# VectorE's two-operand pieces in an image loop, rewritten as scalar_tensor_tensor

## The chip, the cores and the metric

The kernel runs on one NeuronCore of one Trainium2 chip. A core has five engines that run side by side, each through its own list of instructions in order: TensorE (PE, matrix products; PEld is its weight load), VectorE (DVE), ScalarE (ACT), GpSimd (POOL) and SyncE (SP), which here only issues transfers between HBM and the on-chip memory SBUF. TensorE writes its results to a second on-chip memory, PSUM. The metric is the device time of one execution in microseconds, lower is better.

## The reference

Sixteen images of 64 x 64 pixels with 128 channels go through two layers. Layer 0 is a deformable resampling: a group norm, a 3 x 3 convolution that gives two offsets for each channel and pixel, a clip of the resulting coordinates to the image, and a bilinear sample of the normalised image there. Layer 1 is an attention among the 16 numbers of each head of each token, and a mixture of experts whose gate takes the eight best tokens of each of 64 experts.

```python
x = x + conv_ref(_gn(x), L0_conv_W, L0_conv_b)
#   c0 = clip(off[..., 0] + row, 0, 63); c1 = clip(off[..., 1] + col, 0, 63); bilinear sample
t = _to_tokens(x)
t = t + attn_ref(_ln_t(t), w_qkv, b_qkv, w_proj, b_proj)
#   attn = softmax((q * scale)[..., :, None] * k[..., None, :]); out = attn . v, head by head
t = t + ffn_ref(_ln_t(t), gate_w, gate_b, weight1, weight2)
#   softmax over tokens, the 8 best of each expert, two dense layers, added back to those tokens
```

## The kernel before, in words

All arithmetic is in float32, apart from some small bfloat16 pieces of the coordinates. Channels or tokens lie on the 128 partitions. The program is one long piece for the first image, a loop over the fourteen images between (`For_i`, line 1070), a piece for the last image, and then `finish`, which computes the experts and adds their outputs. The change touches only the images' part.

An image is worked in eight strips of 512 pixels. For each strip the following runs:

- `conv(k)` makes the coordinates: 18 matmuls into `cbank` (lines 617 to 623), `coords` adds bias and grid on VectorE (630 to 637), `clip` bounds both coordinates to 0..63 (644), ScalarE and GpSimd split the row coordinate into three bfloat16 parts (645 to 656), and SyncE stores the column coordinate to `cc_d` (646) and the parts to `pc_d` (658).
- `sample` is the heart: 16 steps a strip, 128 an image. In each, SyncE loads `chat` from `cc_d` in four transfers (697), TensorE makes `rps` (719) and ScalarE turns it into row weights `rhat` (728, 729; on VectorE in one step of eight, 726), ScalarE turns `chat` into column weights (708), TensorE makes `yps` in 64 small matmul passes from the image's rows `xr` (739), VectorE multiplies, `product` (745), and TensorE sums into `acc` (751). `yps` has one buffer, so each step's matmuls wait for the product of the step before.
- `tokens` carries a finished strip through the attention: transposes, query, key and value (`qkv`, 852), the extremes of the keys `kmm` (860), GpSimd's `top` and `den` (865), VectorE's maximum `top` (904), GpSimd's `sc` = q k and `sc` - `top` (878, 879), ScalarE's exponential (883), VectorE's sum `den` (885), GpSimd's weighting `ev` (889), VectorE's sum `att` (891). Then comes the projection, a layer norm whose `scale` writes `xln` (782), and the gate.
- `prep` brings in the next image: transposes, group statistics in `gmv` (541 to 551), eight `normalize` pieces that write `pad` (557), differences along the rows, `along` (570, 574), and down the columns, eight `down` pieces that write `xl` (583) and are stored to `xn_d`.
- `tail` treats the image before: the eight best tokens (`best`, 957; `choose`, 969, which is already a scalar_tensor_tensor with both tensor operands in SBUF), their weights, and a running sum copied to `pooled` (1024).

Nothing of this is issued where it is written. Each piece is recorded with a slot number, and `Work.order` (237 to 296) plans one image: it gives each operation an estimated cost (`weight`, 195) and repeatedly takes the operation that can start first, ready ones being ranked by start time plus 150 per slot. What it finds becomes the fixed order of each engine's list. The plan also has a rule for the memory port of VectorE and GpSimd: an operation that `shared` (224) marks starts no earlier than the last planned GpSimd operation ends, and the other way round. Marked are VectorE operations with two wide operands in SBUF, and tensor_scalar and tensor_copy from SBUF to SBUF. Because all the recorded operations are emitted from line 188, the profile shows them all as L188, and they are told apart by the names of their tiles.

Of the kernel before, what the change touches and what calls it, by code (L numbers as in the profile page):

```python
# [44 lines left out]
def bcast(ap, axis, n):  # L45

    shape = list(ap.shape)
    return ap.unsqueeze(axis).to_broadcast(shape[:axis] + [n] + shape[axis:])


def at_image(ap, b):
# [89 lines left out]
class Work:  # L141
# [52 lines left out]
    def weight(self, op):  # L194
        total, cells, shape = 0, {}, None
        for fn, outs, ins in op.operands():
            n = max(a.free_size() for a in outs + ins)
            local = all(a.space == SBUF for a in outs + ins)
            if op.lane == "tensor":
                n = ins[1].free_size() if fn == "matmul" else P  # L200
                n = n * (1 if ins[0].dtype == BF16 else 2 if fn == "transpose" else 4) * 0.4
                shape = (ins[0].partition_size(), outs[0].partition_size())
                part = shape[0] <= 64 and fn == "matmul"
                at = (region(ins[0])[1] if part else 0, region(outs[0])[1])
                cells[at] = cells.get(at, 0) + n + 15
                continue
            if op.lane == "sync":
                total += 100
            elif op.lane == "scalar":
                total += 155 + 0.83 * n + 100 * (len(ins) - 1)  # L210
            elif op.lane == "gpsimd":
                total += 1000 if n <= NA else 150 + (6 if fn == "tensor_scalar" else 1.8) * n
            elif fn == "reciprocal":
                total += 6.5 * n
            elif fn in ("tensor_scalar", "tensor_copy") and local:
                total += 150 + 0.55 * n
            else:
                total += 150 + 1.04 * n
        if op.lane == "tensor":
            wide = shape[1] > 64 or shape[0] > 64 and shape[1] > 32  # L220
            total = sum(cells.values()) if wide else max(cells.values())
        return total, shape

    def shared(self, op):

        if op.lane != "vector":
            return False
        for fn, outs, ins in op.operands():
            wide = [a for a in ins if a.space == SBUF and a.free_size() > 1]
            if len(wide) > 1 or (  # L230
                fn in ("tensor_scalar", "tensor_copy")
                and all(a.space == SBUF for a in outs + ins)
            ):
                return True
        return False
# [66 lines left out]
class Images:  # L302
# [8 lines left out]
    def __init__(self, ctx, tc, x, conv_w, conv_b, w_qkv, b_qkv, w_proj, b_proj, gate_w, gate_b,  # L311
# [63 lines left out]

        self.half = keep([P, NA], "half")
        nc.vector.memset(self.half, -0.5)
        self.one = keep([P, 1], "one")
        nc.vector.memset(self.one, 1.0)

# [124 lines left out]
    def prep(self, b, turns, slot, norm_slot):  # L505
        plan = Work(self.nc, self.tc)
        nc = plan
        xt = at_image(self.x, b).rearrange("b r w c -> (b r w) c").rearrange(
            "(t a p) c -> t p a c", a=NA, p=P)

        def load(t):
            nc.sync.dma_start(self.xl[:, t % 2], xt[t])

        def turn(t):
            for a in range(NA):
                nc.tensor.transpose(
                    self.bank2[:, P * a : P * (a + 1)], self.xl[:, t % 2, a, :], self.ident)

        def stats(t):
            v = self.big[:, CHW * t : CHW * (t + 1)]  # L520
            nc.scalar.copy(v, self.bank2)
            nc.vector.bn_stats(self.gst[:, t, :], v)

        for t, at in enumerate(turns):
            plan.add(at - 3, lambda t=t: load(t))
            plan.together(at + 0.5, lambda t=t: turn(t))
            plan.add(at + 1, lambda t=t: stats(t))

        gmv = self.gmv

        def group1():
            nc.vector.bn_aggr(gmv[:, 0:2], self.gst)

        def group2():
            nc.tensor.matmul(self.bank2[:, 0:2], self.avg, gmv[:, 0:2], start=True, stop=True)

        def group3():
            nc.vector.tensor_copy(gmv[:, 2:4], self.bank2[:, 0:2])  # L540
            nc.vector.tensor_tensor(gmv[:, 0:1], gmv[:, 0:1], gmv[:, 2:3], ALU.subtract)
            nc.vector.tensor_tensor(gmv[:, 1:2], gmv[:, 0:1], gmv[:, 0:1], ALU.mult)

        def group4():
            nc.tensor.matmul(self.bank2[:, 0:1], self.avg, gmv[:, 1:2], start=True, stop=True)

        def group5():
            nc.vector.scalar_tensor_tensor(
                gmv[:, 3:4], self.bank2[:, 0:1], GN_EPS, gmv[:, 3:4], ALU.add, ALU.add
            )  # L550
            nc.gpsimd.tensor_tensor(gmv[:, 3:4], gmv[:, 3:4], self.half[:, 0:1], ALU.pow)

        for i, fn in enumerate((group1, group2, group3, group4, group5)):
            plan.add(slot + i + 0.5 * (i % 2), fn)

        def normalize(t):
            nc.vector.tensor_scalar(
                self.pad[:, 1 + 8 * t : 9 + 8 * t, 1 : 1 + IMG],
                self.big[:, CHW * t : CHW * (t + 1)].rearrange("p (i j) -> p i j", j=IMG),
                gmv[:, 2:3], gmv[:, 3:4], ALU.subtract, ALU.mult,  # L560
            )


        pin = self.pad[:, 1 : 1 + IMG, 1 : 1 + IMG]
        big = self.big.rearrange("p (i j) -> p i j", j=IMG)
        mid = IMG // 2

        def along(s):
            if s == 0:
                nc.vector.tensor_tensor(  # L570
                    big[:, :, : mid - 1], pin[:, :, : mid - 1], pin[:, :, 1:mid], ALU.subtract)
                nc.scalar.copy(big[:, :, mid - 1 : mid + 1], pin[:, :, mid - 1 : mid + 1])
            else:
                nc.vector.tensor_tensor(
                    big[:, :, mid + 1 :], pin[:, :, mid + 1 :], pin[:, :, mid : IMG - 1],
                    ALU.subtract)

        def down(r):
            st = self.xl[:, r % 2].rearrange("p a c -> p (a c)").rearrange(
                "p (i j) -> p i j", j=IMG)  # L580
            lo, hi = 8 * r, 8 * (r + 1)
            last = hi == IMG
            nc.vector.tensor_tensor(
                st[:, : 8 - last], big[:, lo : hi - last], big[:, lo + 1 : hi + 1 - last],
                ALU.subtract)
            for n, w in enumerate(ROW0):
                i0, i1 = max(lo, w), min(hi, w + WIN - 1)
                if i0 < i1:
                    nc.sync.dma_start(
                        self.xn_d[:, i0 - w : i1 - w, n], st[:, i0 - lo : i1 - lo])  # L590
                if lo <= w + WIN - 1 < hi:
                    nc.sync.dma_start(self.xn_d[:, WIN - 1, n], big[:, w + WIN - 1])

        for t in range(NCH):
            plan.add(norm_slot + t // 2, lambda t=t: normalize(t))
            plan.add(norm_slot + 6 + 2 * t, lambda t=t: down(t))
        for s in range(2):
            plan.add(norm_slot + 4 + s, lambda s=s: along(s))
        return plan
# [12 lines left out]
    def conv(self, k, slot):  # L612
# [28 lines left out]
            )  # L641

        def clip():
            nc.vector.tensor_scalar(self.cd, self.cd, 0.0, float(IMG - 1), ALU.max, ALU.min)
            nc.scalar.copy(self.pc[:, 0], self.cd[:, 0])
            nc.sync.dma_start(self.cc_d[k % 2], self.cd[:, 1])

# [120 lines left out]
    def layer_norm(self, src, dst, plan, slot):  # L768
# [10 lines left out]
            nc.gpsimd.tensor_tensor(rstd, rstd, self.half, ALU.pow)  # L779

        def scale(a):
            nc.vector.tensor_scalar(
                dst[:, a, :], src[:, a, :], mv[:, a, 0:1], rstd[:, a : a + 1],
                ALU.subtract, ALU.mult,
            )

        for a in range(NA):
# [7 lines left out]
    def tokens(self, b, k, slot):  # L795
# [14 lines left out]
        def add(rel, fn):  # L810
            plan.add(slot + rel, fn)
# [86 lines left out]
        for a in range(NA):  # L898
# [2 lines left out]
            add(at + 8, lambda: qkv_add(a))  # L901
            add(at + 9, lambda: ends(a))
            add(at + 10, lambda: scores(a))
            add(at + 11, lambda: nc.vector.tensor_tensor(
                tile_of(top, a), tile_of(top, a), tile_of(den, a), ALU.max))
            for i in (2 * a, 2 * a + 1):
                add(12 + 4 * i, lambda: score(i))
                add(14 + 4 * i, lambda: expo(i))
# [42 lines left out]
    def tail(self, b, slot, turns):  # L951
# [3 lines left out]

        def best():
            nc.vector.max(self.top8, logits)
            nc.vector.tensor_scalar(self.ntop, self.top8[:, 0:1], -1.0, None, ALU.mult)

        def expo(k):  # L960
            ks = slice(CHW * k, CHW * (k + 1))
# [56 lines left out]
        def keep(i):  # L1018
# [2 lines left out]
            else:  # L1021
                nc.vector.tensor_tensor(self.pool_sum, self.bank2[:, :E], self.pool_sum, ALU.add)
            if i == NCH // 2 - 1:
                nc.vector.tensor_copy(
                    self.pooled[:, :, b : b + 1] if isinstance(b, int)
                    else self.pooled[:, :, ds(b, 1)], self.pool_sum.unsqueeze(2))

# [247 lines left out]
```

## Time and profile before

| what | value |
| --- | --- |
| median of three runs | 10401.05 us (10379.56 to 10412.2) |
| the profiled execution | 10408.53 us, span 10406.5 us |
| granted TensorE clock, mean | 0.912 |
| one image in the loop | about 611 us |
| VectorE busy | 8475.8 us in 11691 instructions |
| GpSimd busy | 7911.5 us in 5666 instructions |
| `finish`, from about 9900 us on | about 500 us |

How to read the lines: a group line has the source line, the engine, the operation, out<-in by tile names, the shape and count, then after the bar the busy time in us and the mean ns of one, and then the engine's idle time just before such instructions with what ended it. A line of the waits gives the engine and what waited, what it waited for, and then us in total, number and longest. A line of the timeline has the start, the duration, the engine and the instruction. A line of a stretch has its borders and length, then the busy time and count of PE, PEld, DVE, ACT and POOL, the granted clock, the share of the DMA engines and GB/s.

### The profile page before, as it was taken

Reading aid. Unit: us, or ns where it says so; the run is one execution under the profiler, and the core shown is the slowest. Engines: PE = TensorE matmul, PEld = TensorE weight load, DVE = VectorE, ACT = ScalarE, POOL = GpSimd, SP = SyncE. Lnnn points to the kernel's source line nnn. Section 1 sums busy time; section 2 is a strip of 40 time slices with the busy share of each in tenths; the row PEclk is TensorE's granted clock in tenths of the full one; section 3 lists DMA queues with packets and bytes.
Section 4 is the critical chain, followed back from the end, with each engine's and each line's share of the span. In section 5 each row is a group of like instructions: output and inputs, shape, how many; then the busy total and the mean of one; then the engine's idle time right before and its main releaser. Section 6 shows DMA issues by size and latency. Waiting matters only on the chain. (4 is left out here: it accounts for less than half of the span.)

```text
span 10406.5 us, 367626 instructions
## 1 busy us (share of the span) xinstructions
PE 8673.1 (83%) x156228; PEld 4367.3 (42%) x156228; DVE 8475.8 (81%) x11691; ACT 7657.4 (74%) x8034; POOL 7911.5 (76%) x5666
## 2 busy tenths in 40 slices
PE   7978788797878889788888978788897878888567
PEld 3434344343434434343443434344343434434247
DVE  5988889888888988888898888889888888988712
ACT  5878788787878878787887878788787878878500
POOL 3978788787878878787887878788787878878700
PEclk9999899998989999999999999999998999999755
DMA  6565555555555555555555555555555555555277
GB/s 160 160 166 157 159 159 158 160 161 163 158 158 159 153 161 159 163 160 160 158 154 161 159 162 161 158 152 156 164 160 159 162 158 154 157 163 157 79 213 247
DMA packets 1325857, 1672.20 MB, mean 161 GB/s; under 512 B 441632, under 2 KB 658464, under 8 KB 1322080
## 3 DMA queue, kind: packets, MB, share of 16 engines
q1 hardware_dynamic: 1303904, 1613.24, 54.4%
q10 hardware_dynamic: 20224, 34.61, 0.9%
q8 instruction: 1244, 20.38, 0.9%
q14 instruction: 485, 3.97, 0.1%
HBM read 1378.16 MB, written 268.96 MB: 158 GB/s over the span
## 5 line engine op out<-in xcount | busy, mean ns | idle before, releaser
L188 DVE SCALAR_TENSOR_TENSOR prod<-chat,yps 128x1024 f32<-128x1024 f32 x2048 | 2470.7, 1206 | 552.7 <-PE yps L188 254.6
L188 PE MATMUL yps<-rhat,xr 32*32 32x176 f32 (+1 forms) x131072 | 2621.3, 282 | 347.7 <-DVE prod L188 324.8
L188 POOL TENSOR_TENSOR ev<-sc,qkv 128x1024 f32<-128x1024 f32 x1024 | 2429.5, 2373 | 546.3 <-ACT sc L188 484.2
L188 PEld LDWEIGHTS yps<-rhat,xr 32*32 32x32 f32 x131072 | 1860.2, 106 | 1692.0 <-DVE prod L188 926.2
L188 PE MATMUL cbank<-pad,wconv 128*128 128x512 f32 x4608 | 2433.2, 626 | 39.1 <-DVE far L188 15.4
L188 ACT ACTIVATE rhat<-rps 128x1024 f32<-128x1024 f32 x1792 | 1815.9, 1013 | 633.1 <-PE rps L188 526.8
L188 POOL TENSOR_TENSOR sc<-sc,top 128x1024 f32<-128x1024 f32 x1024 | 2010.4, 1963 | 231.6 <-DVE top L188 203.2
L188 ACT ACTIVATE rhat<-rhat,one 128x1024 f32<-128x1024 f32 x1792 | 2057.6, 1148 | 47.1
L188 POOL TENSOR_TENSOR sc<-qkv 128x1024 f32<-128x1024 f32 x1024 | 1987.9, 1942 | 68.9 <-DVE qkv L188 67.6
L188 PE MATMUL rps<-parts,sel 128*128 128x512 bf16 x4096 | 1251.0, 387 | 723.9 <-ACT rhat L188 414.1
L188 DVE TENSOR_REDUCE den<-sc 128x64 f32<-128x1024 f32 x1024 | 1239.8, 1211 | 326.2 <-ACT sc L188 323.0
L188 DVE TENSOR_REDUCE att<-ev 128x64 f32<-128x1024 f32 x1024 | 1233.3, 1204 | 314.1 <-PEq L1070 265.8
L188 ACT ACTIVATE sc<-sc 128x1024 f32<-128x1024 f32 x1024 | 1071.7, 1047 | 497.9 <-PEq L1070 315.1
L188 ACT ACTIVATE chat<-chat,cbi,csc 128x1024 f32<-128x1024 f32 x1024 | 1255.6, 1232 | 125.8 <-DMA chat<-cc_d 108.8
L188 ACT ACTIVATE chat<-chat,cbi 128x1024 f32<-128x1024 f32 x1024 | 1161.4, 1139 | 183.8 <-DMA chat<-cc_d 162.5
L188 PE MATMUL acc<-prod,red 128*32 128x512 f32 x8192 | 1155.4, 629 | 8.5 <-DVE prod L188 8.5
L188 PEld LDWEIGHTS cbank<-pad,wconv 128*128 128x128 f32 x4608 | 828.4, 193 | 692.6 <-issue 468.1
L188 PEld LDWEIGHTS <-sel 128*128 128x128 bf16 x4096 | 334.3, 98 | 1819.4 <-issue 1564.2
L188 POOL TENSOR_TENSOR top<-qkv,kmm 128x128 f32<-128x128 f32 x512 | 226.2, 442 | 692.0 <-POOLq L1070 359.1
L188 DVE TENSOR_SCALAR xln<-t,mv,rstd 128x128 f32<-128x128 f32 x512 | 530.0, 1094 | 41.8 <-POOL rstd L188 41.8
L188 PE MATMUL bank<-wqkv,tr 128*128 128x384 f32 x1024 | 487.3, 561 | 30.8 <-ACT tr L188 18.1
L188 DVE RECIPROCAL den<-den 128x128 f32<-128x128 f32 x512 | 480.0, 937 | 4.5
(143 smaller groups left out, 8134.9 us busy)
## 6 DMA issues: line engine op xcount, KB each, us to landing
chat<-cc_d SPq DMA_DIRECT2D x8192, 128.0 KB
xr<-xn_d SPq DMA_DIRECT2D x512, 128.0 KB
xn_d<-xl SPq DMA_DIRECT2D x192, 256.0 KB
pc_d<-pc SPq DMA_DIRECT2D x128, 384.0 KB
parts<-pc_d SPq DMA_DIRECT2D x768, 64.0 KB
xl<-in_x_dram SPq DMA_DIRECT2D x128, 256.0 KB
xres<-in_x_dram SPq DMA_DIRECT2D x256, 128.0 KB
cc_d<-cd SPq DMA_DIRECT2D x128, 256.0 KB
```

Of the source, the lines that this page charges most:

```text
L188: getattr(engine, fn)(*args, **kwargs)
```

## The change

Every VectorE instruction of the images' loop that reads two tensors from SBUF as a tensor_tensor, or one tensor from SBUF as a tensor_scalar, is written as a scalar_tensor_tensor, (in0 op0 scalar) op1 in1. A new helper `apart` writes a tensor_tensor as (a x 1.0) op b. Where there were two scalars (`normalize`, `clip`, the layer norm's `scale`, `ntop`), one becomes a tensor of step 0: a value of each partition that is repeated, and for the clip a new constant `edge` of 63. The copy to `pooled` goes from VectorE to ScalarE. In the planner, `shared` now marks only a tensor_tensor with two wide operands, and of these the loop has none left; a scalar_tensor_tensor is costed as 150 + 1.04 n, where tensor_scalar from SBUF was 150 + 0.55 n. The new form of ScalarE's cost gives the same numbers for what the loop issues.

```diff
+def apart(nc, out, a, b, op):
+
+    nc.vector.scalar_tensor_tensor(out, a, 1.0, b, ALU.mult, op)
...
-                total += 155 + 0.83 * n + 100 * (len(ins) - 1)
+                total += 155 + 0.83 * n + 100 * sum(a.free_size() == 1 for a in ins)
...
-            if len(wide) > 1 or (
+            if fn == "tensor_tensor" and len(wide) > 1 or (
...
+        self.edge = keep([P, 1], "edge")
+        nc.vector.memset(self.edge, float(IMG - 1))
...
-            nc.vector.tensor_tensor(gmv[:, 0:1], gmv[:, 0:1], gmv[:, 2:3], ALU.subtract)
-            nc.vector.tensor_tensor(gmv[:, 1:2], gmv[:, 0:1], gmv[:, 0:1], ALU.mult)
+            apart(nc, gmv[:, 0:1], gmv[:, 0:1], gmv[:, 2:3], ALU.subtract)
+            apart(nc, gmv[:, 1:2], gmv[:, 0:1], gmv[:, 0:1], ALU.mult)
...
-            nc.vector.tensor_scalar(
+            nc.vector.scalar_tensor_tensor(
                 self.pad[:, 1 + 8 * t : 9 + 8 * t, 1 : 1 + IMG],
                 self.big[:, CHW * t : CHW * (t + 1)].rearrange("p (i j) -> p i j", j=IMG),
-                gmv[:, 2:3], gmv[:, 3:4], ALU.subtract, ALU.mult,
+                gmv[:, 2:3], bcast(gmv[:, 3:4].to_broadcast([P, 8]), 2, IMG),
+                ALU.subtract, ALU.mult,
...
-                nc.vector.tensor_tensor(
-                    big[:, :, : mid - 1], pin[:, :, : mid - 1], pin[:, :, 1:mid], ALU.subtract)
+                apart(
+                    nc, big[:, :, : mid - 1], pin[:, :, : mid - 1], pin[:, :, 1:mid], ALU.subtract)
...
-            nc.vector.tensor_tensor(
-                st[:, : 8 - last], big[:, lo : hi - last], big[:, lo + 1 : hi + 1 - last],
+            apart(
+                nc, st[:, : 8 - last], big[:, lo : hi - last], big[:, lo + 1 : hi + 1 - last],
                 ALU.subtract)
...
-            nc.vector.tensor_scalar(self.cd, self.cd, 0.0, float(IMG - 1), ALU.max, ALU.min)
+            nc.vector.scalar_tensor_tensor(
+                self.cd, self.cd, 0.0, bcast(self.edge.to_broadcast([P, 2]), 2, CHW),
+                ALU.max, ALU.min)
...
-            nc.vector.tensor_scalar(
-                dst[:, a, :], src[:, a, :], mv[:, a, 0:1], rstd[:, a : a + 1],
-                ALU.subtract, ALU.mult,
+            nc.vector.scalar_tensor_tensor(
+                dst[:, a, :], src[:, a, :], mv[:, a, 0:1],
+                rstd[:, a : a + 1].to_broadcast([P, C]), ALU.subtract, ALU.mult,
...
-            add(at + 11, lambda: nc.vector.tensor_tensor(
-                tile_of(top, a), tile_of(top, a), tile_of(den, a), ALU.max))
+            add(at + 11, lambda: apart(
+                nc, tile_of(top, a), tile_of(top, a), tile_of(den, a), ALU.max))
...
-            nc.vector.tensor_scalar(self.ntop, self.top8[:, 0:1], -1.0, None, ALU.mult)
+            nc.vector.scalar_tensor_tensor(
+                self.ntop, self.top8[:, 0:1], -1.0, self.one[:E], ALU.mult, ALU.mult)
...
-                nc.vector.tensor_copy(
+                nc.scalar.copy(
                     self.pooled[:, :, b : b + 1] if isinstance(b, int)
```

More of the change, by code (lines that the diff above doesn't have):

```diff
@@ L569, in along @@
             if s == 0:
-                nc.vector.tensor_tensor(
-                    big[:, :, : mid - 1], pin[:, :, : mid - 1], pin[:, :, 1:mid], ALU.subtract)
+                apart(
+                    nc, big[:, :, : mid - 1], pin[:, :, : mid - 1], pin[:, :, 1:mid], ALU.subtract)
                 nc.scalar.copy(big[:, :, mid - 1 : mid + 1], pin[:, :, mid - 1 : mid + 1])
             else:
-                nc.vector.tensor_tensor(
-                    big[:, :, mid + 1 :], pin[:, :, mid + 1 :], pin[:, :, mid : IMG - 1],
+                apart(
+                    nc, big[:, :, mid + 1 :], pin[:, :, mid + 1 :], pin[:, :, mid : IMG - 1],
                     ALU.subtract)
@@ L582, in down @@
             last = hi == IMG
-            nc.vector.tensor_tensor(
-                st[:, : 8 - last], big[:, lo : hi - last], big[:, lo + 1 : hi + 1 - last],
+            apart(
+                nc, st[:, : 8 - last], big[:, lo : hi - last], big[:, lo + 1 : hi + 1 - last],
                 ALU.subtract)
```

## The prediction

> **What bounds the kernel now.** I read the page first. No engine is full over the span, and four are nearly so:
>
> ```profile
> span 10406.5 us, 367626 instructions
> PE 8673.1 (83%) x156228; PEld 4367.3 (42%) x156228; DVE 8475.8 (81%) x11691; ACT 7657.4 (74%) x8034; POOL 7911.5 (76%) x5666
> ```
>
> The stretch 1000 to 9600 us holds fourteen images of 611 us each; the change touches only this part. There VectorE and TensorE are equally loaded (7,377 and 7,318 us of 8,600):
>
> ```profile
> 1000.00:9600.00 8600.00, 7318.37 (x136354) 3585.46 (x136352) 7377.46 (x10104) 6745.10 (x7068) 6981.58 (x4984) 0.94 0.56 159
> ```
>
> Then the waits, longest first. TensorE waits for VectorE's product (926 and 325 us) and for `xln` (291 and 205 us); GpSimd waits for VectorE's `top` (203 us):
>
> ```profile
> PEld yps L188 <- DVE prod L188: 926.2, 1015, 16.1
> PE yps L188 <- DVE prod L188: 324.8, 478, 15.3
> PEld bank L188 <- DVE xln L188: 290.9, 232, 9.7
> POOL sc L188 <- DVE top L188: 203.2, 356, 2.4
> ```
>
> So no single engine is the bound: a chain that changes engine every few us is. I walked it back from VectorE's last instruction before 9600 us to 1000 us, at each step to what released it: of 8,599 us TensorE holds 2,641, VectorE 2,160, issue 889, DMA 856, ScalarE 846, SyncE's issuing 686, GpSimd 476. VectorE's 2,160 are 29% of its busy time. By tile, the share of the busy time that lies on that walk is 61% for `xln` (304 of 502 us), 79% for `pad` (75 of 95), 55% for the choice `big<-big,logits` (42 of 77), 33% for the clip `cd<-cd` (34 of 104), 18% for `top` (54 of 298) and 14% for `xl` (22 of 158). I use these shares as prices: an added us of a group costs its share.
>
> Last, the groups by shape:
>
> ```profile
> L188 DVE SCALAR_TENSOR_TENSOR prod<-chat,yps 128x1024 f32<-128x1024 f32 x2048 | 2470.7, 1206 | 552.7 <-PE yps L188 254.6 <-ACT rhat L188 69.9 <-ACT chat L188 59.2
> ...
> L188 DVE TENSOR_SCALAR xln<-t,mv,rstd 128x128 f32<-128x128 f32 x512 | 530.0, 1094 | 41.8 <-POOL rstd L188 41.8
> ...
> L188 DVE TENSOR_TENSOR top<-top,den 128x128 f32<-128x128 f32 x512 | 336.6, 657 | 0.0
> ...
> L188 DVE TENSOR_SCALAR cd<-cd 128x1024 f32<-128x1024 f32 x128 | 116.2, 908 | 0.0
> L188 DVE TENSOR_SCALAR pad<-big,gmv 128x512 f32<-128x512 f32 x128 | 97.9, 827 | 0.7 <-POOL gmv L188 0.7
> ...
> L188 DVE SCALAR_TENSOR_TENSOR big<-big,logits 64x512 f32<-64x512 f32 x128 | 84.1, 683 | 0.8 <-ACT logits L188 0.6
> ```
>
> A mean hides two things. I sorted each group by whether a GpSimd instruction overlapped it. With none, `xln` takes 335 ns, `top` 274, the clip 682, `pad` 538, `xl` (the row differences) 685. The rest of the mean is waiting inside the instruction for GpSimd: 0.76 us for each `xln`, 0.38 `top`, 0.23 clip, 0.29 `pad`, 0.79 `xl` (mean 1.477). Times their counts that is 389 + 196 + 29 + 37 + 89 = 740 us.
>
> **Does the new form escape that wait?** The kernel before already has one scalar_tensor_tensor with two SBUF operands, the choice. Two places in the timeline:
>
> ```profile
> 836.49 0.68 DVE L188 SCALAR_TENSOR_TENSOR big<-big,logits 64x512 f32<-64x512 f32 x1
> 836.71 2.26 POOL L188 TENSOR_TENSOR sc<-sc,top 128x1024 f32<-128x1024 f32 x1 [1.04 <-DVE top L188]
> ...
> 2061.37 0.42 POOL L188 TENSOR_TENSOR den<-qkv,kmm 128x128 f32<-128x128 f32 x1
> 2061.39 0.94 DVE L188 SCALAR_TENSOR_TENSOR big<-big,logits 64x512 f32<-64x512 f32 x1
> 2061.73 2.83 POOL L188 TENSOR_TENSOR ev<-sc,qkv 128x1024 f32<-128x1024 f32 x1
> ```
>
> In the first, GpSimd starts 0.22 us behind the choice and takes 2.26 us where its row's median is 1.93: it was held. In the second the choice finds `den` running, takes 0.94 us instead of 0.68, and `ev` takes 2.83 instead of 2.37. Fourteen of the sixteen images repeat the first. The product, with one operand in PSUM, takes 1,205 ns with GpSimd running and 1,211 without: it takes no part. So what collides is the second SBUF operand, whatever the form, and the change keeps it: a normalisation or clip even gains one. I take the wait to stay.
>
> The Trainium skill, "SBUF — State Buffer", section "Who interferes with whom", says a VectorE instruction with two SBUF inputs contends with a GpSimd instruction that reads SBUF. Taken literally it speaks against the change, and the two places agree; but a choice 0.15 us behind the start of GpSimd's 1.04 us `rstd` power took 671 ns, so here the trace is milder than the page. By the page each instruction that met that power would lose up to 0.9 us more, by the row nothing.
>
> **The change part by part.**
>
> Duration without waiting. Subtraction and max (`xl`, `along`, `top`): 685, 2,214 and 274 ns now. The choice's 683 ns at 512 elements and the product's 1,206 at 1024 give 1.02 ns an element and 160 fixed, so 683, 2,185 and 291: nothing within 30 ns. `xln`: the forms with one pointer scalar take 472 ns at 256 elements and 609 at 384, 1.07 an element and 198 fixed, so 335 at 128, as now. The clip now does 1024 elements in 682 ns; the product's form takes 1,206: +0.525 us x 128 = 67 us. `pad`: 198 + 1.07 x 512 = 746 against 538: +0.207 x 128 = 26 us. On the path 67 x 0.33 + 26 x 0.79 = 43 us. The small group statistics (32 and 16 of 0.15 us), `edge` and `pooled` (16 copies of 0.21 us going to ScalarE, 74% busy) are priced at nothing; without that cover they are under 4 us.
>
> The order. VectorE's and GpSimd's planned rows no longer exclude each other. Compared row by row in one image, `top` stands 0.75 products earlier on average, `pad` 1.5, the clip 1.1, the choice 0.75, `xln` 0.62; TensorE's transposes of `xln` move with it. On SyncE the clip's store `cc_d` goes ahead of four column loads that it stood behind, and the loads of `parts` ahead of the first store of the tokens; an issue of that store takes 0.34 us, so four loads come 0.34 us later. They are issued some three slots ahead, and the product waited for them only 29 us in all, so I price that at nothing; without that cover it is 128 x 0.34 = 44 us. Before, `top` mostly has three to nine VectorE instructions between it and its `kmm`; after, eight of 32 have just `att` and a product, so it arrives soon after `den`, when GpSimd's next 1.9 us instruction has begun. The eight `pad` stood together around the clip; after, a product and an `att` stand among them, which keeps GpSimd fed and colliding. Behind a waiting `top` or `pad` stands the next product, and TensorE's 64 `yps` matmuls wait for that.
>
> The trace shows no wait without the plan's avoidance, so I bound it. Low end: unchanged, 0. High end: 1.38 us, what `top` waited in the 51 cases where it came 2.5 to 3 us behind `den` (1.66 in all). I take 0.76, the `xln` row, since `xln` and `xl` (0.79) behave as if unplanned already. Clip (0.76 - 0.23) x 128 x 0.33 = 22 us; `pad` 0.47 x 128 x 0.79 = 48; choice 0.75 x 128 x 0.55 = 53; `top` 0.38 x 512 x 0.18 = 35; `xln`, `xl` nothing. Together 158. GpSimd's own 203 us of waiting for `top` may go with the earlier `top`: at its share of the walk (476 of 6,982, 7%) -14 us; being held longer by clip and `pad` costs 93 x 0.07 = +7.
>
> Sum: 43 + 158 - 7 = +194 us on the profiled execution's 10,408.5, which lies 7.5 above the median 10,401. So 10,595. With the ends of the wait: 43 us (10,444) and, at 1.38 us for clip, `pad`, choice, `top` and also `xln` (0.62 x 512 x 0.61 = 194 us), 43 + 542, 10,986.
>
> **Rivals.** A. The form does escape, because the repeated scalar (step 0) of `xln`, clip and `pad`, unlike the choice's operand, needs no second stream, and the choice is special. Then the waits go: `xln` 389 x 0.61 = 237, `top` 35, `pad` 29, clip 10, `xl` 12, less 43: -280, 10,120. The two places speak against it. It decides once `xln` averages under about 0.7 us. Chance 0.08.
> B. The wait stays but the order is better: `top` and `xln` earlier shorten the image's last strips, whose end the loop's border exposes (attention's row waits 266 us at 13 borders). One product period a image, 4.8 us x 16 = 76, against the 43: 10,370. The dense collisions speak against it. Chance 0.11.
> C. Nothing measurable (a kernel of this kind can be told from no change at about 0.3%, 31 us): added waits fall into VectorE's 14% idle time. Chance 0.08.
> D. Far worse: each `xln` and `pad` alternates with a GpSimd instruction, as at 5417 us, where four `xln` took 6.1 us. 10,800 to 11,000. Chance 0.13.
>
> **How the numbers follow.** My case, slower with 10,440 to 10,800 as its own range, has 0.60. Faster: A 0.08 and B 0.11, 0.19. Same: 0.08. Slower: 0.73. The range runs from 10,340, which takes in B and leaves out A, to 10,850, which takes in part of D.
>
> **What would show it.** Clip near 1.2 us and `pad` near 0.75 in their free cases; `xln` still 0.9 to 1.3 us and `top` risen towards 1 us; the choice above 0.9 us; GpSimd's `sc` and `ev` means not lower; TensorE's waits for `prod` and `xln` larger. I am wrong if minima and means of `top` and `xln` fall together to about 0.3 us.

## The result, and the profile after

The changed kernel takes 10806.17 us in the median of four runs (10802.36 to 10812.68), beside 10396.03 us for the kernel before on the same chip. The ratio is 1.0395, 95% interval [1.0377, 1.0413]: 410 us slower. I had forecast slower, but by less than half of that, 194 us: 10,595, with 10,340 to 10,850 as the range. The measured time lies inside that range, and just above the 10,800 at which I had ended my own case.

The profiled execution took 10812.68 us. The head of its page:

```profile
span 10810.9 us, 366537 instructions
PE 8533.7 (79%) x154709; PEld 4369.4 (40%) x156228; DVE 9096.6 (84%) x11676; ACT 7692.1 (71%) x8050; POOL 8072.9 (75%) x5666
```

Only VectorE has grown much: 621 us more busy time, against 161 us for GpSimd and 35 us for ScalarE, and a span 404 us longer. The groups by shape (mean ns of one behind the busy time) say where the 621 us are:

```profile
L193 DVE SCALAR_TENSOR_TENSOR xln<-t,mv,rstd 128x128 f32<-128x128 f32 x512 | 687.5, 1401 | 1.5 <-POOL rstd L193 1.5
L193 DVE SCALAR_TENSOR_TENSOR top<-top,den 128x128 f32<-128x128 f32 x512 | 582.5, 1138 | 6.7 <-POOL den L193 6.7
L193 DVE SCALAR_TENSOR_TENSOR cd<-cd,edge 128x1024 f32<-128x1024 f32 x128 | 263.8, 2061 | 0.0
L193 DVE SCALAR_TENSOR_TENSOR big<-big,logits 64x512 f32<-64x512 f32 x128 | 184.2, 1439 | 0.8 <-ACT logits L193 0.6
L193 DVE SCALAR_TENSOR_TENSOR pad<-big,gmv 128x512 f32<-128x512 f32 x128 | 142.0, 1151 | 0.7 <-POOL gmv L193 0.7
L193 DVE SCALAR_TENSOR_TENSOR xl<-big 128x512 f32<-128x512 f32 x112 | 100.7, 901 | 2.2 <-DMA xn_d<-xl 2.1
```

Means times counts against before: `top` (0.481 us x 512) +246, `xln` (0.307 x 512) +157, the clip (1.153 x 128) +148, the choice (0.756 x 128) +97, `pad` (0.324 x 128) +41, `xl` (-0.576 x 112) -65. That is 624 of the 621 us.

How much of a mean is waiting I find as before, by sorting on whether a GpSimd instruction overlapped. Undisturbed, `xln` takes 340 ns (144 of them), `top` 281, the clip 1,217 (only 2 of its 128 were undisturbed), the choice 683 (8 of 128), `pad` 743, `xl` 686 (9 of 112). The waiting for GpSimd is therefore 1.06 us for each `xln`, 0.86 `top`, 0.84 clip, 0.76 choice, 0.41 `pad` and 0.21 `xl`. The 361 `xln` that found GpSimd running took 1.81 us on average. One place in the timeline shows it:

```profile
5177.30 1.94 POOL L193 TENSOR_TENSOR sc<-qkv 128x1024 f32<-128x1024 f32 x1
5177.86 6.07 DVE L193 SCALAR_TENSOR_TENSOR xln<-t,mv,rstd 128x128 f32<-128x128 f32 x4
...
5179.18 2.40 POOL L193 TENSOR_TENSOR ev<-sc,qkv 128x1024 f32<-128x1024 f32 x1
...
5181.54 1.98 POOL L193 TENSOR_TENSOR sc<-sc,top 128x1024 f32<-128x1024 f32 x1
...
5183.72 0.45 PEld L193 LDWEIGHTS bank<-ident,xln 128*128 128x128 f32 x2 [1.80 <-DVE xln L193]
...
5184.98 1.21 DVE L193 SCALAR_TENSOR_TENSOR prod<-chat,yps 128x1024 f32<-128x1024 f32 x1
```

Four normalisations whose undisturbed time is 1.4 us last 6.07 us; one by one they take 1.52, 2.43, 2.02 and 0.34 us. The first finds GpSimd's `sc` running, `ev` starts 0.12 us before the second, and the next `sc` 0.11 us before the third. TensorE waits for them three times, and the next product, for which the next 64 `yps` matmuls wait, starts only at 5184.98. The waits sum that up:

```profile
PEld yps L193 <- DVE prod L193: 1327.4, 971, 17.3
PE yps L193 <- DVE prod L193: 808.4, 678, 16.5
PEld bank L193 <- DVE xln L193: 445.3, 314, 9.8
PE bank L193 <- DVE xln L193: 365.8, 254, 9.5
POOL sc L193 <- DVE top L193: 147.4, 223, 1.2
```

TensorE's matmul rows wait 808 us for the product where it was 325, and 366 us for `xln` where it was 205. GpSimd's wait for `top` did shrink, from 203 to 147 us. Walked back as before, VectorE now holds 3,915 of 8,900 us between 1000 and 9900 us, 44%, where it held 2,160 of 8,599, 25%.

### The profile page after: what moved, and what is told of

Same layout as the page of the kernel before. It is cut to its first block, busy times and chain, and to the rows that moved or that the text cites. A ratio compares the mean times of both kernels' runs of the same rounds, so it can differ in the third digit from the quotient of the medians.

```text
span 10810.9 us, 366537 instructions
## 1 busy us (share of the span) xinstructions
PE 8533.7 (79%) x154709; PEld 4369.4 (40%) x156228; DVE 9096.6 (84%) x11676; ACT 7692.1 (71%) x8050; POOL 8072.9 (75%) x5666
## 5 line engine op out<-in xcount | busy, mean ns | idle before, releaser
L193 PE MATMUL cbank<-pad,wconv 128*128 128x512 f32 x4608 | 2463.6, 634 | 145.0 <-DVE far L193 95.3
L193 POOL TENSOR_TENSOR sc<-qkv 128x1024 f32<-128x1024 f32 x1024 | 2047.5, 1999 | 321.0 <-DVE qkv L193 254.5
L193 PE MATMUL rps<-parts,sel 128*128 128x512 bf16 x2577 | 922.4, 391 | 518.7 <-PEq L1081 278.2
L193 ACT ACTIVATE chat<-chat,cbi 128x1024 f32<-128x1024 f32 x1024 | 1163.0, 1140 | 155.9 <-DMA chat<-cc_d 146.6
L193 PE MATMUL acc<-prod,red 128*32 128x512 f32 x8192 | 1188.4, 645 | 37.2 <-DVE prod L193 7.9
L193 DVE SCALAR_TENSOR_TENSOR xln<-t,mv,rstd 128x128 f32<-128x128 f32 x512 | 687.5, 1401 | 1.5 <-POOL rstd L193 1.5
L193 ACT COPY tr<-bank 128x512 f32<-128x512 f32 x384 | 221.5, 577 | 634.4 <-PE bank L193 633.8
L193 DVE SCALAR_TENSOR_TENSOR top<-top,den 128x128 f32<-128x128 f32 x512 | 582.5, 1138 | 6.7 <-POOL den L193 6.7
```

The lines of the kernel that those rows point to most:

```text
L193: getattr(engine, fn)(*args, **kwargs)
```

## The experiments

All are measured against the kernel before on the same chip. The theory was that the port's collisions do it, and that the planner no longer keeps them apart (A). The rival was that the new form itself waits worse (B). A second question came up with the result: what an added us of VectorE time costs.

**Form and order taken apart.** Each recorded operation got a second form that is used only when it is issued, so that the planner sees the one and the chip runs the other. In the first run the plan is that of before and the instructions are the new ones; in the second it is the reverse.

```diff
+    nc.vector.tensor_tensor(
+        out, a, b, op, alt=("scalar_tensor_tensor", (out, a, 1.0, b, ALU.mult, op)))
...
-                getattr(engine, fn)(*args, **kwargs)
+                alt = kwargs.get("alt")
+                if alt:
+                    getattr(engine, alt[0])(*alt[1])
+                else:
+                    getattr(engine, fn)(*args, **kwargs)
```

> Every engine's list in the order of the kernel before; only the instructions are the new forms (ntop and pooled left as they were). Theory A, the loss comes from the plan that no longer keeps VectorE and GpSimd apart: only the longer clip and pad cost, 93 us of VectorE time, 40 to 90 us on the path, 10,440 to 10,490, with xln still near 1.1 us and top near 0.66 us. Theory B, the new form itself waits worse for the port: xln above 1.3 us and top above 1 us here too, 10,650 or more.

Measured: 10456.58 us, ratio 1.0054 [1.004, 1.0068], 54 us. Its `xln`, `top`, `pad`, clip and choice:

```profile
L196 DVE SCALAR_TENSOR_TENSOR xln<-t,mv,rstd 128x128 f32<-128x128 f32 x512 | 479.6, 995 | 22.8 <-POOL rstd L198 22.8
L196 DVE SCALAR_TENSOR_TENSOR top<-top,den 128x128 f32<-128x128 f32 x512 | 350.6, 685 | 0.0
...
L196 DVE SCALAR_TENSOR_TENSOR pad<-big,gmv 128x512 f32<-128x512 f32 x128 | 182.5, 1486 | 0.7 <-POOL gmv L198 0.7
L196 DVE SCALAR_TENSOR_TENSOR cd<-cd,edge 128x1024 f32<-128x1024 f32 x128 | 158.0, 1234 | 0.0
...
L198 DVE SCALAR_TENSOR_TENSOR big<-big,logits 64x512 f32<-64x512 f32 x128 | 124.3, 997 | 0.8 <-ACT logits L198 0.6
```

> The other half: every engine's list in the order of the changed kernel, with the old tensor_tensor and tensor_scalar forms (ntop and pooled stay as changed). Theory A: most of the 410 us is here, 10,700 to 10,770, with xln near 1.4 us and top near 1.1 us although the forms are the old ones. Theory B: near 10,400, with waits as before.

Measured: 10634.75 us, ratio 1.0219 [1.0185, 1.0253], 233 us. The old forms now wait like the new ones:

```profile
L196 DVE TENSOR_SCALAR xln<-t,mv,rstd 128x128 f32<-128x128 f32 x512 | 665.1, 1358 | 1.5 <-POOL rstd L198 1.5
L196 DVE TENSOR_TENSOR top<-top,den 128x128 f32<-128x128 f32 x512 | 572.6, 1118 | 7.6 <-POOL den L198 6.7
L196 DVE TENSOR_SCALAR cd<-cd 128x1024 f32<-128x1024 f32 x128 | 187.6, 1465 | 0.0
```

B falls: in the old order the new `xln` waits 0.66 us, less than the old one did (0.76), `top` waits as long as before, and the clip hardly at all. For these three the long waits belong to the order. `pad` and the choice do wait more in the old order, 0.74 us where it was 0.29 and 0.32 where it was 0.01, although the choice's form is unchanged: an order alone does not fix the moments at which the pieces meet. A was too high on the second run, since 54 + 233 = 287 us, and the two together cost 410. In the new order the longer clip takes 0.53 us more for itself and 0.06 us more waiting, 76 us of VectorE time; the rest of the 120 us I could not place. The granted clock differs too, 0.914 in the second run and 0.908 in the changed kernel (0.912 before), and what that is worth no run tells.

**The planner's rule.** Four runs switch it by parts: put back in the changed kernel; off in the kernel before with its old forms and costs; put back in the changed kernel for `xln` alone, and for `top` alone.

```diff
-            if fn == "tensor_tensor" and len(wide) > 1 or (
+            if len(wide) > 1 or (
...
-            if fn == "tensor_tensor" and len(wide) > 1 or (
+            if len(wide) > 1 and outs[0].tensor.name.startswith('xln') or (
```

> The changed kernel, with the one line of the planner put back that marks every VectorE operation with two wide SBUF operands as holding the port; its cost for the new forms stays. Theory A: the plan avoids collisions again, top back near 0.66 us and the choice near 0.68, 10,430 to 10,550. Theory B: the waits stay as in the changed kernel, 10,700 or more.

> The kernel before, forms and costs unchanged, with the planner's port rule switched off for every operation. If the missing rule alone makes the order's loss (234 us with the old forms in the changed order): 10,600 to 10,680, xln near 1.35 us and top near 1.1 us. If the new costs of clip, pad and xln in the plan make it: near 10,400.

> The changed kernel with the port rule put back for xln alone. xln should fall from 1.40 to about 1.0 us, 205 us of VectorE time; at two thirds 135 us, about 10,670. If xln's neighbours pay instead (top or the choice waiting longer), no gain: 10,800.

> The changed kernel with the port rule put back for top alone. top should fall from 1.14 to about 0.68 us, 235 us of VectorE time; at two thirds 155 us, about 10,650; at the 18% that I priced top with, 42 us, about 10,765.

| run | us | ratio, 95% interval | VectorE busy, us | `xln`, ns | `top`, ns | clip, ns | choice, ns |
| --- | --- | --- | --- | --- | --- | --- | --- |
| before | 10396.03 | 1 | 8475.8 | 1094 | 657 | 908 | 683 |
| changed | 10806.17 | 1.0395 [1.0377, 1.0413] | 9096.6 | 1401 | 1138 | 2061 | 1439 |
| rule back, all but the clip | 10557.71 | 1.0153 [1.0118, 1.0188] | 8707.0 | 1013 | 683 | 2049 | 1036 |
| rule off, old kernel | 10566.79 | 1.0163 [1.0145, 1.018] | 8821.1 | 1267 | 960 | 1499 | 1443 |
| rule back for `xln` | 10627.03 | 1.0224 [1.0206, 1.0242] | 8942.4 | 1064 | 1140 | 1925 | 1444 |
| rule back for `top` | 10715.03 | 1.0306 [1.0288, 1.0324] | 8909.2 | 1480 | 669 | 1728 | 1387 |

The two groups that get the rule back one at a time wait about as little again as in the kernel before, while most others go on waiting:

```profile
L193 DVE SCALAR_TENSOR_TENSOR xln<-t,mv,rstd 128x128 f32<-128x128 f32 x512 | 514.5, 1064 | 1.5 <-POOL rstd L193 1.5
```

```profile
L193 DVE SCALAR_TENSOR_TENSOR top<-top,den 128x128 f32<-128x128 f32 x512 | 342.3, 669 | 0.0
```

The rule for `xln` alone is worth 10806 - 10627 = 179 us, for `top` alone 91 us. Switching it off costs the kernel before 164 us, with no other change:

```profile
L188 DVE TENSOR_SCALAR xln<-t,mv,rstd 128x128 f32<-128x128 f32 x512 | 618.7, 1267 | 5.4 <-POOL rstd L188 5.4
L188 DVE TENSOR_TENSOR top<-top,den 128x128 f32<-128x128 f32 x512 | 491.4, 960 | 8.1 <-POOL den L188 8.1
```

So the missing rule is shown to be a cause, and putting it back returns 248 of the 410 us. 156 us stay. One reason lies in the kernel: the line put back does not reach the clip. The clip writes the tensor that it reads, and `operands` leaves an input out that is the output itself, so the rule sees `edge` as the only wide operand. In the kernel before the clip was marked by the other condition, as a tensor_scalar. It still takes 2.05 us in this run, with 126 of 128 finding GpSimd running; what marking it would give back was not run. `pad` (1.46 us) and the choice (1.04) are marked and still wait more than before. What the new costs of clip, `pad` and `xln` do to the plan's ranking, beyond that, I did not split.

**The price of VectorE's time.** The kernel before, with an extra reduction on VectorE, ahead of the groups that grew. The reduction does not wait for GpSimd: ahead of `top` it takes 463 ns where a GpSimd instruction overlaps it and 473 where none does.

```diff
+                        self.nc.vector.tensor_reduce(
+                            self.idle[1], self.idle[0][:, :n], AX.X, ALU.add)
```

> The kernel before with a reduction of one SBUF tensor (it takes no part in the port) put ahead of each xln, top, clip, choice and pad, as long as what their means grew by in the changed kernel: 0.307, 0.481, 1.152, 0.756 and 0.323 us, 688 us of VectorE time in all. It prices VectorE time alone, with the old waits and no other order. If the shares of the walk were right prices: 96 + 44 + 49 + 53 + 32 = 274 us, about 10,670. If an added us costs two thirds, as 410 us to 621 us in the result: 450 us, about 10,850.

Measured: 10909.24 us, ratio 1.0493 [1.0455, 1.053]: 507 us for a nominal 688, and for 525 us of added busy time (9000.9), partly because `xln` and `xl` waited less than before. The shares of the walk would have made it 274.

> The kernel before with only the reduction of 0.48 us ahead of each top: 512 x 0.48 = 246 us of VectorE time. By the share of the walk that I priced top with, 18%: 44 us, about 10,445. By the price that the run with all five groups lengthened gave (509 us for 688): 180 us, about 10,580.

Measured: 10606.6 us, ratio 1.0199 [1.018, 1.0217]: 204 us.

> The kernel before with the same reduction of 0.48 us ahead of each reciprocal of den, where neither TensorE nor the next GpSimd instruction waits for the result at once. If VectorE's time costs 0.8 to 0.9 wherever it is put, because the next product comes later: 190 to 210 us, about 10,600, as with top. If the 200 us came from top's own place (GpSimd's sc waiting for it): clearly less, 10,450 to 10,520. The walk gave the reciprocal 111 us of some 424 in its stretch, 26%, which would be 62 us.

Measured: 10510.65 us, ratio 1.0107 [1.009, 1.0124]: 103 us. The reduction's group, first of the run ahead of `top`, then of the run ahead of `den`:

```profile
L195 DVE TENSOR_REDUCE idle<-wconv 128x1 f32<-128x324 f32 x512 | 238.4, 466 | 0.0
```

```profile
L190 DVE TENSOR_REDUCE idle<-wconv 128x1 f32<-128x324 f32 x512 | 241.5, 472 | 0.0
```

And two of their waits, in the same order:

```profile
PE yps L197 <- DVE prod L197: 445.0, 492, 14.7
POOL sc L197 <- DVE top L197: 266.5, 397, 2.8
```

```profile
PE yps L192 <- DVE prod L192: 447.7, 584, 16.5
POOL sc L192 <- DVE top L192: 238.3, 375, 3.2
```

The same 240 us cost 0.86 of themselves ahead of `top` and 0.43 ahead of the reciprocal. In both, TensorE's wait for the product grows by some 120 us, and GpSimd's wait for `top` too, by 63 and 35 us. The walk had put 18% of `top` and 26% of the reciprocal on the path. It understates both.

The granted clock is not the same in these runs: 0.894 with all five groups, 0.903 ahead of `top`, 0.913 ahead of the reciprocal, 0.912 before. Without the `rps` matmuls, of which some records are missing, TensorE is busy 128 us longer than before in the first, 56 us longer in the second and 26 us shorter in the third. Even if all of that is taken out of the times, the first costs some 380 us where the shares gave 274, and the other two 0.62 and 0.53 of their reduction. So the shares are too low either way; that a place ahead of `top` is dearer than one ahead of the reciprocal is not shown.

**A version that beats both.** If `xln` on VectorE collides, it can leave VectorE. ScalarE makes it as rstd x + (-mean rstd).

```diff
+            if dst is not None:
+                nc.gpsimd.tensor_scalar(self.off, mv[:, :, 0], -1.0, None, ALU.mult)
+                nc.gpsimd.tensor_tensor(self.off, self.off, rstd, ALU.mult)
...
-            nc.vector.tensor_scalar(
-                dst[:, a, :], src[:, a, :], mv[:, a, 0:1], rstd[:, a : a + 1],
-                ALU.subtract, ALU.mult,
-            )
+            nc.scalar.activation(
+                dst[:, a, :], src[:, a, :], AF.Identity, bias=self.off[:, a : a + 1],
+                scale=rstd[:, a : a + 1])
```

> The kernel before with xln made on ScalarE, as rstd x + (-mean rstd), where two small GpSimd instructions make the second term; nothing else changes. VectorE loses 512 instructions of 1.09 us mean (0.34 without waiting), 560 us, and GpSimd meets VectorE's port less; ScalarE gains 512 of about 0.3 us, 150 us, and GpSimd 128 x about 0.5 = 64 us. If VectorE's time costs 0.8 as in the run with top lengthened: up to 400 us less, about 10,050 to 10,150. If it costs only what the walk gave for xln, and ScalarE's addition as much again as its share: about 200 us less, 10,200. If ScalarE (74% busy) becomes the bound: no gain, 10,400.

Measured: 10203.55 us, ratio 0.9816 [0.9794, 0.9837]: 194 us faster than the kernel before, near the second of the three cases. The head of its page, the new group, and a wait:

```profile
span 10186.5 us, 368249 instructions
PE 8544.1 (84%) x156228; PEld 4307.9 (42%) x156228; DVE 7964.0 (78%) x11179; ACT 7832.9 (77%) x8546; POOL 7964.2 (78%) x5922
```

```profile
L188 ACT ACTIVATE xln<-t,off,rstd 128x128 f32<-128x128 f32 x512 | 209.4, 480 | 8.1 <-POOL off L188 7.6 <-issue 0.5
```

```profile
PEld bank L188 <- ACT xln L188: 50.1, 107, 6.2
```

VectorE gives up 512 us, ScalarE takes on 176, GpSimd 53. The activation takes 0.48 us where I had put 0.3. TensorE's weight loads wait 50 us for `xln` where they waited 291. A price of 0.8 would have meant 400 us for the 512; it was 0.38, net of what the other two engines took on, at a granted clock of 0.922 in the profiled run beside 0.912 before.

## Why the prediction was right or wrong, point by point

**No single engine bounds it; a chain does.** Held: VectorE's busy time rose by 7%, the time by 4%, and TensorE's matmuls waited 484 us longer for the product and 160 us longer for `xln`.

**The new form does not escape the wait.** Right, and now shown. The undisturbed times are 340 ns for `xln`, 281 for `top`, 1,217 for the clip and 743 for `pad`, as worked out (335, 291, 1,206, 746). Where GpSimd was running at the start, in the same order, the new `xln` took 1.81 us and the old one 1.75, the new `top` 1.39 and the old one 1.41. An operand of step 0 collides too, so rival A of the prediction is gone. That the second SBUF operand is what collides, as the prediction puts it, is too narrow: the old `xln` and clip, with one wide SBUF operand, wait in the same way (in that order 1.75 us against 0.34 undisturbed, and 1.48 against 0.68).

**Clip and `pad`, 43 us.** Near the 54 us of the new forms in the old order, but in part by luck. Of the 70 us of added busy time there, the clip has 42 and not 67, because it waited less, `pad` 84 and not 26 and the choice 40 because they waited more, and `xln` and `xl` gave back 110; and the shares were no prices, as said below.

**The wait without the plan's avoidance, 0.76 us.** Near for three groups: 0.86 `top`, 0.84 clip, 0.76 choice. Too much for `pad` (0.41). Wrong for `xln`, which the sum put at nothing: the step says `xln` and `xl` "behave as if unplanned already". The plan had protected `xln` after all; in the new order the wait went from 0.76 to 1.06 us, in the old forms as well (1.358 - 0.335 = 1.02), with the rule alone switched off it was 0.93, and putting the rule back for `xln` is worth 179 us. The mean of 1.40 us lies above the 0.9 to 1.3 that I gave as a sign. `xl` went the other way, from 0.79 to 0.21.

**The step that failed most: "an added us of a group costs its share".** Put the measured growth of every group into my own sum, at my shares, and it gives 157 x 0.61 + 246 x 0.18 + 148 x 0.33 + 97 x 0.55 + 41 x 0.79 - 65 x 0.14 = 96 + 44 + 49 + 53 + 32 - 9 = 265 us. So better waits would have moved the forecast from 194 to some 260, above all by the 96 us of `xln`, which the sum had at nothing. Of the remaining 145 us I hold the price to be the larger part, because the run that put the same five lengths into the old order cost 507 us where the shares gave 274. How the 145 split between the price, the order and the clock no run tells. The share of a group that lies on one walk says how much of it was last to end in this execution, and not what more of it will cost. `top` shows it most: priced at 0.18, while its reduction cost 0.86 of itself, or 0.62 with all of the clock's difference taken out. In the changed kernel the walk, from 1000 to 9900 us, holds 242 us of `top` where it held 54, and 139 of the clip where it held 34. Why is argued, not shown: in the loop four engines are 78 to 86% busy and alternate every few us, so what is not on the walk may follow it by less than the added time and come onto it. A walk of the lengthened kernels does not bear this out, since it holds only 37 of 211 us of the reduction ahead of `top` and 42 of 214 ahead of the reciprocal.

**GpSimd's gain of 14 us.** Its wait for `top` fell by 56 us, not 203; the effect on the time was not measured apart.

**The rivals of the prediction.** B, a better order, is refuted by the run of the old forms in the new order. C, nothing measurable, is refuted by the result. D, `xln` alternating with GpSimd, happened in part (a row of four takes 5.4 us on average, 4.1 before), and the time came out at D's lower end, 10,806.

## What to carry to other kernels

A change of instruction form does not free a shared port if the operands still come through it: look for an instruction of the new form that the kernel already has, and read its time beside the other engine's. When a planner keeps two engines apart, its rule is part of the performance, and must describe what the chip does, not what the change hopes for; when the rule is changed, list which operations it marks. Price added time on a nearly full engine by a run that adds it, and read the granted clock beside it. A share of one walk through the trace is no price: here it was too low by a factor of 1.6 and 4.8 where a reduction was added, and too high where `xln` left VectorE (0.61 against 0.38, net of what the other engines took on).

## What the runs showed of the hardware that I had not expected

An instruction whose second operand is of step 0 in SBUF, one value repeated, collides with GpSimd like one with two full tensors: in the changed kernel `xln` takes 340 ns undisturbed and 1,810 ns on average where GpSimd is running, `top` 281 and 1,394. In a row of such instructions GpSimd often gets in between. Of the 128 rows of four `xln`, the second took over 0.6 us in 112, the third in 96, the fourth in 17; in the row shown, four `xln` of 1.4 us in all took 6.07 us around GpSimd instructions of 2.40 and 1.98 us that started just before the second and the third.
